# Layer norms with tokens on partitions, and the output product of a second attention taken token by token, in a two-layer transformer block

## The chip, the cores and the metric

The kernel runs on one core of a Trainium2 chip. The metric is the device time of one execution in microseconds (us). An execution with the hardware profiler gives a trace of every instruction on every engine: TensorE (PE, its weight loads PEld), VectorE (DVE), ScalarE (ACT), GpSimd (POOL) and SyncE (SP), which issues transfers.

## The reference, cut to what matters

The input is 4 sequences of 1024 tokens with 128 features. Two layers follow, each `x = x + attention(norm(x)) * silu(feedforward(norm(x)))`, all in fp32:

```
def _layernorm(x, axis=-1, eps=1e-05):
    m = jnp.mean(x, axis=axis, keepdims=True)
    v = jnp.var(x, axis=axis, keepdims=True)
    return (x - m) / jnp.sqrt(v + eps)
...
    xn = _layernorm(x, axis=-1)
    s = _L0_attn_ref(xn, L0_attn_w_kqv)
    g = _silu(_L0_ffn_ref(xn, ...))
    x = x + s * g
    xn = _layernorm(x, axis=-1)
    s = _L1_attn_ref(xn, ...)
    g = _silu(_L1_ffn_ref(xn, ...))
    x = x + s * g
```

The first attention has 16 heads of 8 features and a window of 64 tokens. The first feed-forward mixes the weights of eight experts, per sequence, by a gate that is averaged over the sequence. The second attention runs over the four sequences: each of the 1024 positions has a softmax over 4 tokens t and s per head, and a gated relative bias. The second feed-forward has two input products of 512, two inner products of 512 x 512 and an output product.

## The kernel before

The features lie on the 128 partitions and the tokens along the free axis, so x, its norm xn and all intermediate results are [128, tokens] tiles. A unit u is 512 tokens; there are eight, two for each sequence b.

The program order at the end of `block_kernel` is: the norms of units 0 and 1 and the experts of sequence 0; then for each unit the first attention (four blocks of 128 tokens, each in four groups of four heads), the first feed-forward `ffn0`, the norm for the second layer, and a generator `ffn1` for the second feed-forward, which advances a step at every yield of the next unit's attention. In unit 0 the norms of the other sequences and their experts stand between the blocks. Last comes `attend`, the second attention, in two halves n of 512 positions: its first half advances the last unit's `ffn1`, its second has nothing beside it.

A scheduler, when the program is built, places the instructions of each engine in an order of its own, by estimated costs and data dependencies; the order is fixed from then on, and each engine works through its own in order. Tiles come from pools with a fixed number of buffers: in PSUM four banks "M", two "S", one "T" and one "O"; in SBUF four buffers of every tag of `tmp`, `t2k` among them.

Lines that matter:

- `layernorm`, L153 to L177: centring by a product with I - 1/128 (L156), the square (L158), the copy of the centred values (L160), four products with a column 1/128 that give the variances with tokens on partitions (L163), square root (L165) and reciprocal (L167), a diagonal matrix of the reciprocals made by POOL (L169), its product with ones, which repeats a token's factor on every partition (L176), and the last product (L177).
- `experts`, L179 to L206: the gate (L185, L187, its sum L189) and 16 mixing steps of DVE (L206).
- `attention`: scores (L250), bias (L258), maximum (L262), subtraction on POOL (L263), Exp (L264), totals (L265), transposes (L268), their copy (L270), product with the values (L273).
- `ffn0`: residual on POOL (L303, L304). `ffn1`: L312, L313, the inner products L323, the output product L329, its result into g1 (L330).
- `attend`: projections (L341), gate (L352), scores over 32 partitions per token t (L381), softmax (L392 to L399), the expansion of the probabilities (L409), which reads 32 partitions of t and writes 128, product with the values (L412, L415), sum over s on POOL (L416), output projection (L420), bias and gate (L422), residual (L423), transfer out (L424).
- The transfers at the start (L111 to L124): on SP the constants, the gate, the expert weights tw1, then x1 to x3 and wa; on ACT x0, the attention bias, w1, w2 and tw2.

An fp32 matmul of the program is two MATMUL records of the trace.

Of the kernel before, what the change touches and what calls it, by code (L numbers as in the profile page):

```python
# [27 lines left out]
C_ID, C_CEN, C_ONE, C_AVG, C_MP, C_MF, C_SEL, C_EXP = np.cumsum(  # L28
    [0, 128, 128, 128, 1, 4, 512, 64]
).tolist()  # L30
# [12 lines left out]
def constants():  # L43
# [4 lines left out]
    c[:, C_CEN:C_CEN + P] = np.eye(P) - 1.0 / P  # L48
    c[:, C_ONE:C_ONE + P] = 1.0
    c[:, C_AVG] = 1.0 / P  # L50
# [20 lines left out]
def block_kernel(ctx: ExitStack, tc: tile.TileContext, a: dict, out: bass.AP):  # L71
# [12 lines left out]
    def t2k(tag="t2k"):  # L84
        return tmp.tile([P, 512], F32, tag=tag, name=tag)
# [5 lines left out]
    x = [main.tile([P, S], F32, tag=f"x{b}", name=f"x{b}") for b in range(B)]  # L91
    cst = const.tile([P, C_N], F32, tag="cst", name="cst")
# [19 lines left out]
    nc.scalar.dma_start(out=x[0], in_=a["x"][:, 0:S])  # L112
# [9 lines left out]
    for b in range(1, B):  # L122
        nc.sync.dma_start(out=x[b], in_=a["x"][:, b * S:(b + 1) * S])
# [19 lines left out]
    g1 = main.tile([P, B, S], F32, tag="g1", name="g1")  # L143
# [9 lines left out]
    def layernorm(u):  # L153
        b, cx, cn = tokens(u)
        xc_ps = bank()
        PE.matmul(xc_ps, lhsT=cst[:, C_CEN:C_CEN + P], rhs=x[b][:, cx], start=True, stop=True)  # L156
        sq = t2k()
        ACT.activation(sq, xc_ps, AF.Square)  # L158
        xc = t2k()
        DVE.tensor_copy(xc, xc_ps)  # L160
        var = bank()
        for i in range(4):
            PE.matmul(var[:, i:i + 1], lhsT=sq[:, i * P:(i + 1) * P], rhs=cst[:, C_AVG:C_AVG + 1], start=True, stop=True)  # L163
        std = small([P, 4], "std")
        ACT.activation(std, var[:, 0:4], AF.Sqrt, bias=eps)  # L165
        rstd = small([P, 4], "rstd")
        DVE.reciprocal(rstd, std)  # L167
        diag = t2k()
        POOL.tensor_tensor(  # L169
            diag.rearrange("p (i c) -> p i c", i=4),  # L170
            ident.unsqueeze(1).to_broadcast([P, 4, P]),
            rstd.unsqueeze(2).to_broadcast([P, 4, P]),
            ALU.mult,
        )
        rep = bank()
        PE.matmul(rep, lhsT=ones, rhs=diag, start=True, stop=True)  # L176
        DVE.tensor_tensor(xn[b][:, cn], xc, rep, ALU.mult)  # L177
# [155 lines left out]
    def attend(n, pool):  # L333
# [67 lines left out]


        acc = pool.tile([P, B, U], F32, tag="aq", name="acc")
        for s in range(B):
            eps4 = [bank() for _ in range(B)]
            for half in range(2):
                for t in range(B):
                    rows = slice(32 * t, 32 * t + 32)
                    PE.matmul(eps4[t][:, half * hu:(half + 1) * hu], lhsT=expand[rows, half, :], rhs=pr[rows, s, :], start=True, stop=True)  # L409
            for t in range(B):  # L410
                if s == 0:
                    DVE.tensor_tensor(acc[:, t, :], eps4[t], vv[:, s, :], ALU.mult)  # L412
                else:
                    pv = pool.tile([P, U], F32, tag="pd", name="pd", bufs=8)
                    DVE.tensor_tensor(pv, eps4[t], vv[:, s, :], ALU.mult)  # L415
                    POOL.tensor_tensor(acc[:, t, :], acc[:, t, :], pv, ALU.add)  # L416
            yield
        for t in range(B):
            op = bank("O")
            PE.matmul(op, lhsT=wa[:, 3 * D:4 * D], rhs=acc[:, t, :], start=True, stop=True)  # L420
# [7 lines left out]
    for u in range(2):  # L428
        layernorm(u)
# [14 lines left out]
    for u in range(8):  # L444
        q, k, vv = nxt
        s = at.tile([P, U], F32, tag="s", name="s", bufs=2)
        for t in range(4):
# [3 lines left out]
            if u == 0 and t < 3:  # L451
                for i in range(2):
                    layernorm(2 * (t + 1) + i)
                experts(t + 1)
# [10 lines left out]
        layernorm(u)  # L465
# [72 lines left out]
```

## Time and profile before

| | |
|---|---|
| runs | 2259.92, 1119.83, 1118.67 us; median 1119.83 |
| profiled execution, own time | 2259.92 us (the first of these runs) |
| its span, first to last instruction | 2258.1 us |
| mean granted TensorE clock in it | 1.000 |
| transfers over the span | 14.80 MB |
| ACT table loads | 183 in the program's order, 1.28 us each |

The profiled execution took about twice as long as the two others. Times of rows and stages below are those of the profiled execution; the median is that of the runs.

How to read the profile: its first part gives each engine's busy time, its share of the span and the number of instructions. The chain that ended last follows the work back from the last instruction, at each step to what released it. A row of a group has the line, the engine, the operation, "output<-input" by the program's names, shapes, the number of instructions, then busy time in us and the mean duration in ns, then the idle time of the engine just ahead of them and what ended it. Busy time counts overlapping instructions once, so busy time divided by the number is the time that one occupies. A stage row has its stretch, then busy time and number of instructions of PE, PEld, DVE, ACT and POOL, the granted clock, the transfer engines' share and GB/s. A timeline row has its start, its duration, and in brackets the idle time before it with its releaser.

### The profile page before, as it was taken

To read this page: it belongs to the slowest core of one execution; us is meant where nothing else is said; L and a number is where in the kernel's file an instruction comes from. 1 tells how busy PE (TensorE), PEld (TensorE's weight loads), DVE (VectorE), ACT (ScalarE), POOL (GpSimd) and SP (SyncE) were. 2 spreads that over 40 slices of the span, in tenths; PEclk is the share of its full clock that TensorE was granted. 3 is DMA by queue.
4 is the path that set the end of the run, shared out by engine and by line. 5 is a ranking of instruction groups with operands and counts; after the bars stand their busy time and mean duration, and the time that the engine had idled before them with its cause. 6 is when DMAs were issued, how large, how long until landed. Compare 5 with 4: busy or idle time off the path is not lost.

```text
span 2258.1 us, 11983 instructions
## 1 busy us (share of the span) xinstructions
PE 2173.7 (96%) x4760; PEld 813.0 (36%) x4760; DVE 440.9 (20%) x726; ACT 541.6 (24%) x709; POOL 365.9 (16%) x364
## 2 busy tenths in 40 slices
PE   6998999999999999999999999999999999989995
PEld 3345342343334342334324333434334433332322
DVE  2343411112011201111011201121111201113124
ACT  1221322222122313222122312232222312211010
POOL 2310301022011201121101200120102110011223
DMA  4000100000000000000000000000000000000000
GB/s 161 1 0 0 52 0 0 0 0 0 0 0 0 0 0 0 0 0 1 0 0 0 0 0 1 0 0 0 0 0 1 0 0 0 0 0 0 0 19 19
DMA packets 3959, 14.80 MB, mean 7 GB/s; under 512 B 568, under 2 KB 824, under 8 KB 3264
## 3 DMA queue, kind: packets, MB, share of 16 engines
q1 hardware_dynamic: 3184, 9.85, 1.1%
q10 hardware_dynamic: 720, 4.19, 0.5%
q8 instruction: 37, 0.61, 0.1%
q14 instruction: 18, 0.15, 0.0%
HBM read 11.95 MB, written 2.10 MB: 6 GB/s over the span
## 4 chain that ended last, share of the span: by engine, by line
PE 93%; DVE 2%; POOL 2%; issue 1%; ACT 1%; DMA 0%; POOLq 0%; ACTq 0%; DVEq 0%
PE ps_M L323 27%; PE ps_S L250 15%; PE ps_O L273 12%; PE ps_T L268 6%; PE ps_M L312 3%; PE ps_M L329 3%; PE ps_M L300 3%; PE ps_M L296 3%; PE ps_M L313 3%; PE ps_M L341 3%; PE ps_M L176 2%; PE ps_M L226 2%; PE ps_M L156 1%; PE ps_M L163 1%; PE ps_M L409 1%
## 5 line engine op out<-in xcount | busy, mean ns | idle before, releaser
L323 PE MATMUL ps_M<-hid,l1h 128*128 128x512 f32 x512 | 632.4, 1416 | 0.0
L250 PE MATMUL ps_S<-kb,q 32*64 32x512 f32 x512 | 349.9, 1365 | 21.0 <-DVE pr L258 15.6
L273 PEld LDWEIGHTS ps_O<-pt,vb 128*32 128x32 f32 x2048 | 249.0, 170 | 283.1 <-issue 241.2
L273 PE MATMUL ps_O<-pt,vb 128*32 128x64 f32 x2048 | 307.6, 369 | 12.0 <-ACT pt L270 8.0
L258 DVE TENSOR_TENSOR pr<-ps_S,bias 128x512 f32<-128x512 f32 x128 | 87.4, 686 | 1086.8 <-PE ps_S L250 1071.3
L323 PEld LDWEIGHTS ps_M<-hid,l1h 128*128 128x128 f32 x512 | 159.9, 332 | 316.8 <-issue 311.3
L263 POOL TENSOR_TENSOR pr<-pr,mx 128x512 f32<-128x512 f32 x128 | 132.3, 1040 | 737.3 <-DVE mx L262 727.0
L324 ACT ACTIVATE hid<-ps_M,vec 128x512 f32<-128x512 f32 x64 | 44.0, 687 | 551.5 <-PE ps_M L323 551.5
L268 PE MATMUL ps_T<-cst,pr 128*128 128x128 f32 x512 | 173.5, 503 | 1.8 <-ACT pt L270 1.8
L268 PEld LDWEIGHTS ps_T<-cst,pr 128*128 128x128 f32 x512 | 95.0, 207 | 168.7 <-issue 153.2
L270 ACT COPY pt<-ps_T 128x512 f32<-128x512 f32 x128 | 74.9, 585 | 297.8 <-PE ps_T L268 288.0
L264 ACT ACTIVATE pr<-pr 128x512 f32<-128x512 f32 x128 | 79.3, 627 | 203.0 <-POOL pr L263 202.8
L242 POOL TENSOR_TENSOR vb<-v,cst 128x512 f32<-128x512 f32 x64 | 72.5, 1150 | 237.8 <-PE ps_O L273 171.9
L233 POOL TENSOR_TENSOR kb<-k,cst 128x768 f32<-128x768 f32 x32 | 46.8, 1469 | 374.5 <-PE ps_S L250 308.3
L250 PEld LDWEIGHTS ps_S<-kb,q 32*64 32x64 f32 x512 | 29.5, 134 | 212.8 <-issue 132.4
L264 ACT ACT_TABLE_LOAD x82 | 105.2, 1283 | 1.4
L265 DVE TENSOR_REDUCE total<-pr 128x4 f32<-128x512 f32 x128 | 85.3, 679 | 73.9 <-ACT pr L264 73.9
L262 DVE TENSOR_REDUCE mx<-pr 128x4 f32<-128x512 f32 x128 | 86.1, 682 | 10.7 <-POOL pr L260 4.0
L313 PE MATMUL ps_M<-xn,l1w 128*128 128x512 f32 x64 | 84.7, 1425 | 0.0
L312 PE MATMUL ps_M<-xn,l1w 128*128 128x512 f32 x64 | 82.8, 1396 | 0.0
L329 PE MATMUL ps_M<-hid,l1w 128*128 128x512 f32 x64 | 78.2, 1416 | 0.0
L296 PE MATMUL ps_M<-xn,mw 128*128 128x512 f32 x64 | 78.0, 1440 | 0.0
(112 smaller groups left out, 1321.6 us busy)
## 6 DMA issues: line engine op xcount, KB each, us to landing
tw<-in_tw SPq DMA_DIRECT2D x1, 2048.0 KB, 11.8
tw<-in_tw ACTq DMA_DIRECT2D x1, 2048.0 KB, 14.4
l1h<-in_l1h SPq DMA_DIRECT2D x2, 1024.0 KB, 8.5
out<-t2k SPq DMA_DIRECT2D x8, 256.0 KB, 2.0
x<-in_x SPq DMA_DIRECT2D x3, 512.0 KB, 13.0
bias<-in_bias ACTq DMA_DIRECT2D x1, 1024.0 KB, 8.3
l1w<-in_l1w SPq DMA_DIRECT2D x3, 256.0 KB, 2.9
cst<-in_const SPq DMA_DIRECT2D x1, 610.5 KB, 5.8
```

The lines of the kernel that those rows point to most:

```text
L250: PE.matmul(sp[W * i:W * i + W, :, :], lhsT=q[rows, t * P + W * i:t * P + W * i + W], rhs=kb[rows, :, W * i:W * i + P], start=True, stop=True,
L258: DVE.tensor_tensor(pr, sp, bias[:, 4 * j:4 * j + 4, :], ALU.add)
L262: DVE.tensor_reduce(mx, pr, AX.X, ALU.max)
L263: POOL.tensor_tensor(pr, pr, mx.unsqueeze(2).to_broadcast([P, 4, P]), ALU.subtract)
L264: ACT.activation(pr, pr, AF.Exp)
L268: PE.transpose(tp[:, h, :], pr[:, h, :], ident)
L273: PE.matmul(o[rows, W * i:W * i + W], lhsT=vb[i][:, h, rows], rhs=pt[:, h, W * i:W * i + W], start=(h == 0), stop=(h == 3),)
L296: PE.matmul(hp, lhsT=mw1[b][:, c * P:(c + 1) * P], rhs=xn[b][:, cn], start=True, stop=True)
L312: PE.matmul(p1, lhsT=wt["w1"][:, c * P:(c + 1) * P], rhs=xn[b][:, cn], start=True, stop=True)
L313: PE.matmul(p2, lhsT=wt["w2"][:, c * P:(c + 1) * P], rhs=xn[b][:, cn], start=True, stop=True)
L323: PE.matmul(hp, lhsT=wt[name][:, i, c * P:(c + 1) * P], rhs=hid[:, i, :], start=(i == 0), stop=(i == FC - 1))
L329: PE.matmul(op, lhsT=wt["w3"][:, i, :], rhs=hid[:, i, :], start=(i == 0), stop=(i == FC - 1))
```

## The change

There are two parts. The layer norm first. The input norm (units 0 to 7 of the first layer) reads a second copy of x with tokens on partitions, `xt`, which the host prepares and which is loaded into the tile g1, whose own contents are written only later. The norm between the layers turns x by four TensorE transposes into one M bank. Both then take batch-norm statistics and their aggregation on DVE, square root on ACT, reciprocal and normalisation on DVE, four transposes back into one bank, and a copy to xn on ACT. The centring, variance and diagonal products, the square and POOL's diagonal go.

The second part is in `attend`: the loop over the tokens t is now outside that over s. For each pair, two expansions of the same 32 partitions are followed by the product with the values and an output projection of this product, which accumulates over s in PSUM. The accumulator in SBUF and POOL's additions go, and with them four of the yields.

```
+    g1 = main.tile([P, B, S], F32, tag="g1", name="g1")
+    xt = [g1[:, b, :].rearrange("p (i d) -> p i d", d=P) for b in range(B)]
...
-    nc.scalar.dma_start(out=x[0], in_=a["x"][:, 0:S])
+    nc.scalar.dma_start(out=g1[:, 0, :], in_=a["xt"][:, 0:S])
...
     for b in range(1, B):
+        nc.sync.dma_start(out=g1[:, b, :], in_=a["xt"][:, b * S:(b + 1) * S])
+    for b in range(B):
         nc.sync.dma_start(out=x[b], in_=a["x"][:, b * S:(b + 1) * S])
...
-    def layernorm(u):
+    def layernorm(u, src):
+        b, _, cn = tokens(u)
+        stats = small([P, 4, 6], "stats")
+        mv = small([P, 4, 2], "mv")
+        for i in range(4):
+            DVE.bn_stats(stats[:, i, :], src[:, i, :])
+        for i in range(4):
+            DVE.bn_aggr(mv[:, i, :], stats[:, i, :])
         std = small([P, 4], "std")
+        ACT.activation(std, mv[:, :, 1], AF.Sqrt, bias=eps)
         rstd = small([P, 4], "rstd")
         DVE.reciprocal(rstd, std)
+        nt = t2k()
+        nt = nt.rearrange("p (i d) -> p i d", i=4)
+        for i in range(4):
+            DVE.tensor_scalar(nt[:, i, :], src[:, i, :], mv[:, i, 0:1], rstd[:, i:i + 1], ALU.subtract, ALU.mult)
+        back = bank()
+        for i in range(4):
+            PE.transpose(back[:, i * P:(i + 1) * P], nt[:, i, :], ident)
+        ACT.copy(xn[b][:, cn], back)
+
+    def layernorm_in(u):
+        layernorm(u, xt[u // 2][:, 4 * (u % 2):4 * (u % 2) + 4, :])
+
+    def layernorm_mid(u):
+        b, cx, _ = tokens(u)
+        turned = bank(shape=(P, 4, P))
+        for i in range(4):
+            at = cx.start + i * P
+            PE.transpose(turned[:, i, :], x[b][:, at:at + P], ident)
+        layernorm(u, turned)
...
-        acc = pool.tile([P, B, U], F32, tag="aq", name="acc")
-        for s in range(B):
-            eps4 = [bank() for _ in range(B)]
-            for half in range(2):
-                for t in range(B):
-                    rows = slice(32 * t, 32 * t + 32)
-                    PE.matmul(eps4[t][:, half * hu:(half + 1) * hu], lhsT=expand[rows, half, :], rhs=pr[rows, s, :], start=True, stop=True)
-            for t in range(B):
-                if s == 0:
-                    DVE.tensor_tensor(acc[:, t, :], eps4[t], vv[:, s, :], ALU.mult)
-                else:
-                    pv = pool.tile([P, U], F32, tag="pd", name="pd", bufs=8)
-                    DVE.tensor_tensor(pv, eps4[t], vv[:, s, :], ALU.mult)
-                    POOL.tensor_tensor(acc[:, t, :], acc[:, t, :], pv, ALU.add)
-            yield
         for t in range(B):
+            rows = slice(32 * t, 32 * t + 32)
             op = bank("O")
-            PE.matmul(op, lhsT=wa[:, 3 * D:4 * D], rhs=acc[:, t, :], start=True, stop=True)
+            for s in range(B):
+                ep = bank()
+                for half in range(2):
+                    PE.matmul(ep[:, half * hu:(half + 1) * hu], lhsT=expand[rows, half, :], rhs=pr[rows, s, :], start=True, stop=True)
+                pv = pool.tile([P, U], F32, tag="pd", name="pd", bufs=8)
+                DVE.tensor_tensor(pv, ep, vv[:, s, :], ALU.mult)
+                PE.matmul(op, lhsT=wa[:, 3 * D:4 * D], rhs=pv, start=(s == 0), stop=(s == B - 1))
```

The built order after the change has, in the first half of `attend`, four expansions of one token, two projections, and again four and two, with four matmuls of L323 between tokens; in the second half expansions and projections alone. It has 175 ACT table loads. On DVE the statistics of units 2 to 4, which read xt1 and xt2, stand ahead of the gate's sum of sequence 0.

## The prediction

> **What bounds the kernel now.** I read the times, the busy shares, a table of five stages, the chain that ended last, the groups by shape, then the timeline of the last 40 us. First lines of the page:
>
> ```profile
> span 2258.1 us, 11983 instructions
> PE 2173.7 (96%) x4760; PEld 813.0 (36%) x4760; DVE 440.9 (20%) x726; ACT 541.6 (24%) x709; POOL 365.9 (16%) x364
> PE 93%; DVE 2%; POOL 2%; issue 1%; ACT 1%; DMA 0%; POOLq 0%; ACTq 0%; DVEq 0%
> ```
>
> In this execution TensorE is the bound almost everywhere. But it took 2259.92 us, and two other runs of the program took 1119.83 and 1118.67. DVE, ACT and POOL sum to 1348 us, overlapped, so half the time can only come from the matmuls: with r the share of their profiled durations that the shorter runs need, 2173.7 r must fit into 1118.67, so r is at most 0.515. Every sum is made twice, in the profile's time and in the median's.
>
> Stages, from the stage table (stretch, PE busy, PE weight loads, DVE, ACT, POOL):
>
> ```profile
> 38.00:238.00 200.00, 183.92 (x566) 95.80 (x567) 87.84 (x156) 45.85 (x77) 43.97 (x44) 1.00 0.00 1
> 238.00:2040.00 1802.00, 1774.73 (x3748) 646.93 (x3750) 280.49 (x470) 468.15 (x595) 260.08 (x263) 1.00 0.01 2
> 2040.00:2190.00 150.00, 149.98 (x248) 45.39 (x240) 36.95 (x48) 17.92 (x23) 31.33 (x24) 1.00 0.02 7
> 2190.00:2258.00 68.00, 43.31 (x169) 14.79 (x168) 30.78 (x40) 3.87 (x5) 26.54 (x21) 1.00 0.04 16
> ```
>
> They are: the first unit with six layer norms and three experts; seven units of attention and feed-forward; second attention's first half, mixed with feed-forward; its second half, alone. With PE times r the first is close to DVE's 88 us, the second and third stay TensorE's with idle gaps, and the last is a chain.
>
> [...] The trace has two records per fp32 matmul (512 at L323 for 256 in the program)[...]. I take r = 0.40, with 0.35 and 0.515 as ends. [...] an L409 record, four row groups in turn, occupies 28.5/128 = 0.22 us, and L219, full height, 23.1/32 = 0.72 us for 288 columns. [...]
>
> **The change part by part.** Price rows:
>
> ```profile
> L156 PE MATMUL ps_M<-x,cst 128*128 128x512 f32 x32 | 42.1, 1407 | 10.4 <-DMA x<-in_x 6.8 <-POOL x L304 3.5
> L176 PE MATMUL ps_M<-t2k,cst 128*128 128x512 f32 x32 | 41.9, 1411 | 6.5 <-POOL t2k L169 6.5
> L163 PE MATMUL ps_M<-cst,t2k 128*128 128x1 f32 x128 | 38.0, 418 | 4.4 <-ACT t2k L158 4.4
> L268 PE MATMUL ps_T<-cst,pr 128*128 128x128 f32 x512 | 173.5, 503 | 1.8 <-ACT pt L270 1.8
> L219 PE MATMUL ps_M<-xn,wqkv 128*128 128x288 f32 x32 | 23.1, 905 | 0.0
> L409 PE MATMUL ps_M<-apr,cst 32*128 32x256 f32 x128 | 28.5, 805 | 9.2 <-DVE apr L399 8.4 <-DVE acc L412 0.9
> L420 PE MATMUL ps_O<-acc,wa 128*128 128x512 f32 x16 | 21.2, 1425 | 5.5 <-DVE t2k L422 2.8 <-POOL acc L416 2.7
> ```
>
> *Layer norm.* Out: (42.1 + 41.9 + 38.0)/16 = 7.6 us of PE each. In: four transposes at 173.5/512 = 0.34, so 1.4 us, for each of eight input norms; eight, 2.7 us, for each of eight middle norms. PE saves 6.2 and 4.9 us. DVE loses a copy, a reciprocal and a product (0.685 + 0.171 + 0.688 = 1.54) and gains four statistics, four aggregations, a reciprocal and four normalisations. The trace shows no batch-norm instruction: a statistic lies between L435's 0.15 (eight elements) and L289's 0.29 (128), I take 0.28 because it reads 128; an aggregation 0.16; a normalisation 0.28 (L191 0.274). Sum 3.05, so DVE +1.5 us, ends +1 and +1.6. ACT swaps a square (0.60) for a copy (0.59) and has eight table loads fewer (183 to 175, 1.28 each); POOL loses 1.04. The chain from x to xn has two hops fewer and about equal work; I give it nothing. A middle norm keeps one M bank until its last normalisation; other users of M in that stretch wait for xn anyway.
>
> *Waits added.* In each middle norm the statistics wait on DVE for PE's transposes, which wait for POOL's residual add; behind them stand a maximum and two totals of attention, for which POOL's subtraction and PE's transposes wait. Before, the copy L160 stood in that queue with the same wait, so the wait is moved and not new; only its length (eight short instructions against one) is, and it is in the 1.5 us. The result's copy now waits on ACT for four transposes; behind it stands a copy of attention's transposed weights, for which PE's L273 waits. Before, L158's square stood there with a wait of its own. In second attention a projection waits on PE for DVE's product (0.69) right behind the expansions: one or two more expansions stand between, 0.5 us or more at r = 0.40, so a few tenths per pair are open, inside the 1 us of the tail and the range.
>
> *Head.* SP issues three xt loads where x1 to x3 stood, then four x loads, 2 MB more, needed first at the residual add (261 us in the profile); only wa is behind them, needed after 2000 us. The DVE order puts statistics of xt1 ahead of the first normalisation, and x1 landed at 17.3 us: first xn near 20 us, gate sum near 27 against 35.5 us. Profile -7.6; at r = 0.40 the old chain ends near 24, the new near 23: -1.
>
> *First unit.* Six norms: PE -37 in the profile. At r = 0.40 PE saves 15 but DVE, as busy there, gains 9, partly under waits that go: -3, ends -12 and +9.
>
> *Middle norms.* Eight times -4.9 = -39; at r = 0.40 -15.7, of which I count -12 since PE idles there part of the time; ends -24 and -4.
>
> *Second attention, per half.* The expansion's 64 records lose their neighbours in other row groups, the token's loop now being outermost: 64 x 0.642 (L219 scaled to 256 columns) = 41.1 against 14.2, +26.9. The output projection goes from 4 to 16 matmuls: 24 records more at 1.325, +31.8. POOL loses 12 adds of 1.27 us, DVE nothing. First half: +58.7; at r = 0.40 +23.5, less about 2 that L420 waits for the adds: +21. The order keeps feed-forward matmuls between tokens; gaps could take more.
>
> *Second half.* Old, from the timeline:
>
> ```profile
> 2221.28 2.60 PE L409 MATMUL ps_M<-apr,cst 32*128 32x256 f32 x16 [8.38 <-DVE apr L399]
> 2228.35 14.71 POOL L416 TENSOR_TENSOR acc<-acc,pd 128x512 f32<-128x512 f32 x12 [22.92 <-DVE pd L415]
> 2239.46 2.63 PE L420 MATMUL ps_O<-acc,wa 128*128 128x512 f32 x2 [2.67 <-POOL acc L416]
> 2253.75 1.26 POOL L423 TENSOR_TENSOR t2k<-t2k,x 128x512 f32<-128x512 f32 x1 [2.34 <-DVE t2k L422]
> ```
>
> From probabilities to the end: 36.8 us. The reader sees POOL's adds carry it, which do not shrink with r: 4.3 + 14.7 + a projection 1.06 + 0.75 + 1.26 + 3.1 to the end = 25-26. New: PE carries it: 64 x 0.642 + 32 x 1.325 = 83.5, and about 5 after the last matmul: 88.5, +51.7 in the profile; at r = 0.40 33.4 + 1 + 5.1 = 39.5, +13. VectorE's 16 products (11 us) hide under it.
>
> Sum in the profile: -7.6 - 37 - 39 + 58.7 + 51.7 = +27, 2260 to 2287. At r = 0.40: -1 - 3 - 12 + 21 + 13 = +18, 1119.8 to **1138**. Own range 1124 to 1152.
>
> **The rivals.** *Gaps take it.* TensorE is the bound of the profiled execution only; at 0.35 it is busy 761 us of 1119, so the first half's extra fits gaps (+8), the tail costs +10, middle norms give all of -24 with the shorter chain, the first unit -12, the head -2: 1100. Against: the third stage has 150 us of PE beside at most 37 of any other engine. *The serial product is fully exposed.* One mechanism, in second attention: r near 0.5, no gap free: +29 and, with the old tail at 28.5 and the new at 48, +19; the norms return only -5 and -1: 1162. It decides once PE in the shorter runs exceeds about 0.45 of the profile's; for it, the chain's 93%. *VectorE becomes the bound.* Thirteen short instructions in order ahead of attention's products: first unit +9, middle norms -4, head -1, attention +34: 1158. Against: DVE is busy 280 of 1802 us in the middle. That the change does not do what it says is excluded for the order of instructions, which is fixed at build: four matmuls of one token stand together, then two projections.
>
> **How the numbers follow.** Forecast 0.48, gaps 0.15, serial 0.22, VectorE 0.15. Two per cent, about what a measurement of this kernel can tell from no change, is 1097 to 1142. Faster: half of gaps, 0.07. Slower: 0.15 of the forecast's 0.48, 0.20 of serial, 0.09 of VectorE, 0.44. Same: 0.49. The range takes in gaps and serial with their bounds: 1104 to 1172.
>
> **What would show it.** Right: expansion records about 0.64 us apart if matmuls take as long as in this profile, about 0.26 at r = 0.40, against 0.22 now; no POOL add in the tail; the tail from probabilities near 40 us; statistics near 0.28. Wrong: expansions of different tokens overlapping, the statistics holding DVE's queue before attention's products, the xt wait starting the gate later than before, or r outside 0.35 to 0.515.

## The result, and the profile after

The changed kernel takes 1132.48 us (median of 4 runs, 1127.72 to 1134.09) against 1119.25 beside it (median of four, the run of 2259.92 us among them): a ratio of 1.0114, 95% interval 1.0075 to 1.0152. It is slower, by less than the two per cent that count as a difference. The forecast was 1138. The ratios are estimated from the single runs and are not quotients of the medians.

Two things have to be known before the numbers are read. The profile of before was taken in an execution of twice the usual time; the kernel before was therefore run again (first experiment below), and stages are compared with that profile, whose span is 1118.3 us. And the mean clock granted to TensorE differs between executions of one kernel, from 0.865 to 0.883 of full speed in that repeat, and the time goes with it, 1126 down to 1109 us; so a difference of a few us in a long stage that TensorE fills is not read as an effect of the edit.

The page of the changed kernel, the same three lines as in the prediction (span, busy time, chain that ended last):

```profile
span 1130.4 us, 11985 instructions
PE 1001.9 (89%) x4712; PEld 492.7 (44%) x4712; DVE 459.1 (41%) x886; ACT 523.5 (46%) x701; POOL 331.3 (29%) x324
issue 5%; POOL 1%; POOLq 0%
```

TensorE is busy 89% of the span. The chain says nothing this time: it breaks off after the last 6%. So the stages have to carry the comparison. Stage table of the changed kernel (columns as in the prediction: stretch, PE, PE weight loads, DVE, ACT, POOL, granted clock):

```profile
20.30:149.00 128.70, 98.59 (x529) 59.49 (x529) 95.60 (x215) 37.63 (x73) 41.85 (x38) 0.70 0.12 50
149.00:937.60 788.60, 738.88 (x3598) 356.50 (x3598) 275.83 (x522) 441.54 (x569) 251.53 (x249) 0.90 0.00 1
1001.70:1048.10 46.40, 46.31 (x129) 23.04 (x130) 14.11 (x21) 3.35 (x4) 5.06 (x4) 0.96 0.06 21
1083.30:1130.40 47.10, 41.11 (x96) 19.82 (x96) 14.03 (x21) 0.00 (x0) 5.06 (x4) 0.75 0.06 23
```

The same four stretches of the kernel before, run again:

```profile
26.60:163.80 137.20, 105.67 (x578) 61.19 (x576) 84.71 (x155) 46.53 (x79) 43.09 (x43) 0.75 0.00 1
163.80:951.20 787.40, 747.20 (x3627) 359.34 (x3626) 274.84 (x462) 440.81 (x569) 254.56 (x257) 0.90 0.01 4
1020.20:1045.60 25.40, 22.91 (x97) 10.35 (x98) 9.95 (x17) 3.34 (x4) 13.48 (x11) 0.93 0.00 1
1084.70:1118.30 33.60, 21.19 (x72) 11.46 (x72) 12.94 (x20) 0.00 (x0) 19.73 (x16) 0.50 0.08 31
```

They are the first unit, seven units, the first half of second attention from its probabilities, and the second half from its probabilities. The first is 8.5 us shorter, the second the same although TensorE is busy 8 us less, the third 21.0 longer and now full of TensorE, the fourth 13.5 longer. Where each us went, with three of the experiments beside it (us from one event to the next, worked out from the traces):

| stage | before again | after | norms alone | attention alone | input norms alone |
|---|---|---|---|---|---|
| start to the first gate product | 26.6 | 20.3 | 20.5 | 26.9 | 20.6 |
| to the first `ffn0` | 137.2 | 128.7 | 127.4 | 137.0 | 124.7 |
| seven units, to the last `ffn0` | 787.4 | 788.6 | 781.1 | 784.0 | 783.7 |
| to the gate of second attention | 42.3 | 37.5 | 37.5 | 42.3 | 39.8 |
| to the probabilities, first half | 26.7 | 26.6 | 26.7 | 26.6 | 26.7 |
| to the end of the last `ffn1` | 25.4 | 46.4 | 25.4 | 46.4 | 23.7 |
| to the gate of the second half | 13.7 | 10.2 | 13.6 | 10.2 | 13.7 |
| to its probabilities | 25.4 | 25.0 | 25.4 | 25.0 | 25.4 |
| to the end | 33.6 | 47.1 | 33.4 | 47.3 | 33.4 |

The gains lie at the start (-6.3 and -8.5) and before second attention (-4.8); the losses in second attention (+21.0 - 3.5 - 0.4 + 13.5). With +1.2 in the units that is +12, the difference of the two spans. The row of the seven units shows how far a long stage can be trusted: "after" and "norms alone" do the same work there and take 788.6 and 781.1 us, at mean clocks of 0.90 and 0.91.

Four of the price rows in the kernel before, run again (busy time, mean ns of one):

```profile
L323 PE MATMUL ps_M<-hid,l1h 128*128 128x512 f32 x512 | 248.5, 613 | 1.6 <-DVE acc L412 0.8
L156 PE MATMUL ps_M<-x,cst 128*128 128x512 f32 x32 | 30.0, 1037 | 16.2 <-POOL x L304 9.5
L409 PE MATMUL ps_M<-apr,cst 32*128 32x256 f32 x128 | 19.6, 550 | 10.7 <-DVE apr L399 9.5 <-DVE acc L412 0.8
L420 PE MATMUL ps_O<-acc,wa 128*128 128x512 f32 x16 | 12.3, 861 | 6.3 <-POOL acc L416 3.5 <-DVE t2k L422 2.8
```

Rows of the changed kernel that answer the price rows:

```profile
L172 PE MATMUL ps_M<-cst,t2k 128*128 128x128 f32 x64 | 21.1, 418 | 20.5 <-DVE t2k L169 20.5
L185 PE MATMUL ps_M<-cst,x 128*128 128x128 f32 x32 | 7.9, 394 | 10.0 <-POOL x L313 10.0
L159 DVE BATCH_NORM_STATS2 stats<-g 128x6 f32<-128x128 f32 x32 | 7.3, 272 | 15.9 <-DMA g<-in_xt 15.9
L416 PE MATMUL ps_M<-apr,cst 32*128 32x256 f32 x128 | 36.8, 447 | 9.5 <-DVE apr L408 9.5
L419 PE MATMUL ps_O<-pd,wa 128*128 128x512 f32 x64 | 39.0, 737 | 0.8 <-DVE pd L418 0.8
```

The statistic takes 272 ns; it overlaps its neighbours and occupies 7.3/32 = 0.23 us, where 0.28 was forecast. With all that VectorE does in a norm, it is busy 2.77 us per norm instead of 1.53, so +1.2 where +1.5 was forecast. An expansion record occupies 36.8/128 = 0.29 us; in the kernel before, run again, it was 19.6/128 = 0.15. These averages mix two halves with different clocks. In the first half, at stage clocks of 0.93 and 0.96, it went from 0.10 to 0.25 us, close to the forecast's scaled 0.09 and 0.26; in the second, at 0.50 and 0.75, from 0.20 to 0.32. Its neighbours no longer work in other row groups (in the first profile 59 of the 128 records of L409 start within 0.015 us of the one before; those of L416 in the first half mostly start 0.22 us apart). Of the 64 records of the projection 48 are new work; they occupy 0.61 us each on average, and follow each other by 0.43 where the clock is full.

The last 47 us of the changed kernel in the timeline, first token (start, duration):

```profile
1083.40 2.92 PE L416 MATMUL ps_M<-apr,cst 32*128 32x256 f32 x6 [8.37 <-DVE apr L408]
1086.25 2.08 PE L419 MATMUL ps_O<-pd,wa 128*128 128x512 f32 x2
```

There is no POOL sum any more (the stage row shows POOL with the 4 residuals alone, 5.06 us); TensorE goes from expansion to projection. But the two records of a projection take 2.08 us here, and in the first half about 1.0. The clock of 0.75 is a mean: it is 0.50 in this trace until 1106.7 us, for almost half of the stage, and 1.00 from there to the end. The records tell the same: projection records that follow each other directly start 0.85 us apart up to then, and 0.43 afterwards.

### The profile page after: what moved, and what is told of

Same layout as the page of the kernel before. It is cut to its first block, busy times and chain, and to the rows that moved or that the text cites. A ratio compares the mean times of both kernels' runs of the same rounds, so it can differ in the third digit from the quotient of the medians.

```text
span 1130.4 us, 11985 instructions
## 1 busy us (share of the span) xinstructions
PE 1001.9 (89%) x4712; PEld 492.7 (44%) x4712; DVE 459.1 (41%) x886; ACT 523.5 (46%) x701; POOL 331.3 (29%) x324
## 5 line engine op out<-in xcount | busy, mean ns | idle before, releaser
L332 PE MATMUL ps_M<-hid,l1h 128*128 128x512 f32 x512 | 246.4, 609 | 0.0
L259 PE MATMUL ps_S<-kb,q 32*64 32x512 f32 x512 | 184.2, 726 | 35.1 <-DVE pr L267 24.4
L282 PEld LDWEIGHTS ps_O<-pt,vb 128*32 128x32 f32 x2048 | 137.4, 122 | 125.6 <-issue 51.1
L282 PE MATMUL ps_O<-pt,vb 128*32 128x64 f32 x2048 | 163.8, 240 | 21.5 <-ACT pt L279 21.4
L332 PEld LDWEIGHTS ps_M<-hid,l1h 128*128 128x128 f32 x512 | 88.8, 190 | 99.5 <-issue 94.0
L251 POOL TENSOR_TENSOR vb<-v,cst 128x512 f32<-128x512 f32 x64 | 84.9, 1352 | 98.5 <-PE ps_O L282 74.9
L277 PE MATMUL ps_T<-cst,pr 128*128 128x128 f32 x512 | 99.4, 323 | 3.6 <-ACT pr L273 3.6
L277 PEld LDWEIGHTS ps_T<-cst,pr 128*128 128x128 f32 x512 | 68.8, 162 | 67.9 <-issue 41.2
L242 POOL TENSOR_TENSOR kb<-k,cst 128x768 f32<-128x768 f32 x32 | 46.6, 1467 | 152.1 <-PE ps_S L259 111.3
L416 PE MATMUL ps_M<-apr,cst 32*128 32x256 f32 x128 | 36.8, 447 | 9.5 <-DVE apr L408 9.5
L418 DVE TENSOR_TENSOR pd<-ps_M,av 128x512 f32<-128x512 f32 x32 | 22.1, 692 | 48.3 <-PE ps_M L416 48.3
## 6 DMA issues: line engine op xcount, KB each, us to landing
x<-in_x SPq DMA_DIRECT2D x4, 512.0 KB, 12.6
```

The lines of the kernel that those rows point to most:

```text
L251: POOL.tensor_tensor(m, vv[:, 2 * t + i, :].unsqueeze(1).to_broadcast([P, 4, D]), mfree, ALU.mult)
L259: PE.matmul(sp[W * i:W * i + W, :, :], lhsT=q[rows, t * P + W * i:t * P + W * i + W], rhs=kb[rows, :, W * i:W * i + P], start=True, stop=True,
L277: PE.transpose(tp[:, h, :], pr[:, h, :], ident)
L282: PE.matmul(o[rows, W * i:W * i + W], lhsT=vb[i][:, h, rows], rhs=pt[:, h, W * i:W * i + W], start=(h == 0), stop=(h == 3),)
L332: PE.matmul(hp, lhsT=wt[name][:, i, c * P:(c + 1) * P], rhs=hid[:, i, :], start=(i == 0), stop=(i == FC - 1))
```

## The experiments

Ratios are to the kernel before, run in the same job, with the 95% interval. Of each edit a few lines are shown, with "..." for others; "-" and "+" are against the kernel before or the changed kernel, as each case says.

**The kernel before again** (no edit). 

> The kernel before, unchanged, for a profile of an execution that takes about as long as the median. Forecast's theory: about 1119 us, fp32 matmul records of 512 columns 429 ns apart where the first profile had 1106 (as in the kernel after), the tail from the probabilities to the end 25 to 26 us and carried by the additions on GpSimd, a gap at TensorE ahead of each middle norm. Rival that gaps take it: TensorE idle well over 20 us in second attention's first half. Rival that the serial product is fully exposed: almost no idle time there.

1124.65 us (18 runs), ratio 1.0025 [0.9984, 1.0065]. Nothing of the double time of the first execution came back; a record of the inner products of `ffn1` (L323) occupies 248.5/512 = 0.485 us in it instead of 632.4/512 = 1.235. For this line the share r that the forecast worked with is therefore 0.39, where 0.40 was taken; over all of TensorE it is 991.5/2173.7 = 0.456. TensorE is idle 2.5 of the 25.4 us of second attention's first half, so there are no gaps for the rival *Gaps take it* to fill. The tail was expected to take 25 to 26 us and takes 33.6.

**The norms alone.** The new norms, second attention as before (against the changed kernel):

```
-            for s in range(B):
-                ep = bank()
...
+        acc = pool.tile([P, B, U], F32, tag="aq", name="acc")
+        for s in range(B):
+            eps4 = [bank() for _ in range(B)]
```

> Only the layer norms changed, second attention as before. Forecast's theory (TensorE saves 16 us of the path): 1103 us, that is 0.986 of before. Rival that VectorE becomes the bound: +4 us, 1123. Rival that gaps take it: norms give 38 us, 1081. Serial rival: norms return only 6, 1113.

1092.47 us, ratio 0.9771 [0.9716, 0.9826]: faster than before by 1.7 to 2.8%. This lies between the forecast's theory (1103) and the rival of the gaps (1081), and rules out the other two (1113 and 1123). The norms gain more than the forecast's 16 us. By the stage table 15.9 us are gained up to the first `ffn0`, 4.8 after the last, and 6.3 in the seven units; of those 6.3 the clock can make as much as the whole, since the changed kernel, with the same norms, gains nothing there.

**Second attention alone.** The old norms, the new `attend` (against the kernel before):

```
-        acc = pool.tile([P, B, U], F32, tag="aq", name="acc")
-        for s in range(B):
...
+                PE.matmul(op, lhsT=wa[:, 3 * D:4 * D], rhs=pv, start=(s == 0), stop=(s == B - 1))
```

> Only second attention's output changed, the layer norms as before. Forecast's theory: +34 us, 1153. Rival that gaps take it: +18, 1137. Rival that the serial product is fully exposed: +48, 1167. VectorE rival: +34. If the two parts are independent, this difference and that of the norms alone add up to the +13 of the whole change.

1149.84 us, ratio 1.0314 [1.0221, 1.0407]: +25 to +46 us, so the forecast's +34 holds and the +18 and +48 of two rivals do not. The two parts of the change add up within these intervals: -2.3% and +3.1% against +1.1% together. Stage by stage the changed kernel is the norms-alone column up to second attention, apart from the seven units, and the attention-alone column from there.

**The order alone.** Second attention token by token, but with POOL's sum and one projection per token (against the kernel before):

```
+        for t in range(B):
+            rows = slice(32 * t, 32 * t + 32)
+            op = bank("O")
...
+                    POOL.tensor_tensor(acc, acc, pv, ALU.add)
+            PE.matmul(op, lhsT=wa[:, 3 * D:4 * D], rhs=acc, start=True, stop=True)
```

> The kernel before with one thing changed in second attention: the token's loop is outermost, so that expansions of the same 32 partitions follow each other, but the sum over s stays on GpSimd and there is one output projection for each token. First half (from the probabilities to the end of feed-forward's output product): old 25.4 us; 64 expansion records one after another at 216 ns, as in the kernel after, in place of groups of four: about +7, so 32. Tail: old 33.6; 64 records in a row beside the additions, about 34 if TensorE's clock stays low there, 28 if the projections now overlap the additions. Whole: +7 (1127), or +1 with the shorter tail. Rival that the order alone carries the loss: +20 or more. Rival that gaps take it: 0.

**The projections alone.** The loop over s outside and the row groups side by side as before, but each product goes straight into the projections, which add up in four PSUM banks (against the kernel before):

```
+        ops = [bank("O"), bank("T"), bank("S"), bank("S")]
...
-                    POOL.tensor_tensor(acc[:, t, :], acc[:, t, :], pv, ALU.add)
+                PE.matmul(ops[t], lhsT=wa[:, 3 * D:4 * D], rhs=pv, start=(s == 0), stop=(s == B - 1))
```

> The kernel before with the other thing changed: s stays outermost, expansions of four row groups together, but each product goes straight into an output projection that accumulates in one of four PSUM banks (O, T and both S), with no sum on GpSimd. First half: 12 more projections at 0.86 us: +10, less 3.5 for the projections that no longer stand among the next half's input projections: +7 in all. Tail: old 33.6; if TensorE's clock stays as low as in the old tail (0.5), 16 projections of 2.05 us give about 40; if it recovers, 16 at 0.86 and the expansions give about 25. Whole: from -2 to +13, 1118 to 1133. Rival that the projections carry the whole loss of the change in second attention: +30.

The order alone: 1138.36 us, ratio 1.0161 [1.0083, 1.0240]. The projections alone: 1132.40 us, ratio 1.0106 [1.0050, 1.0161]. The last stage of the order alone:

```profile
1096.40:1137.20 40.80, 32.23 (x72) 19.69 (x72) 13.83 (x21) 0.00 (x0) 20.19 (x16) 0.50 0.07 26
```

and of the projections alone:

```profile
1094.30:1126.40 32.10, 22.18 (x96) 9.93 (x96) 12.66 (x20) 0.00 (x0) 4.93 (x4) 0.82 0.09 33
```

So in the last stage the loss needs the order: 33.6 to 40.8 us with 72 records as before, and 47.1 with projections and order together; the projections by themselves cost nothing there (32.1 us), although they are 24 records more. They take the place of POOL's sum, and the stage was granted 0.82 of the clock instead of 0.50; how much each of the two does is not separated. In the first half, where other matmuls are waiting, both cost: 25.4 to 44.0 us with the order, to 37.3 with the projections, to 46.4 with both; 3.4 to 3.5 us of this come back in the next stage each time. An expansion record occupies 0.28 us there with the order alone and 0.10 with the projections alone, so its price is the order's. The two losses do not add. With the order alone the projections also wait for POOL's sums, which accumulation in PSUM takes away, but only for 2.4 us in this half; its clock there was 0.81 instead of 0.96, and what makes the rest is not settled. The order was expected to cost 7 us and cost 18 by the ratio; the projections were expected between -2 and +13, and cost 12.

**The input norms alone.** The norm between the layers as before, the input norms new (the tile of the statistics with two buffers; against the kernel before):

```
     for u in range(2):
-        layernorm(u)
+        layernorm_in(u)
...
         ffn0(u, s)
-        layernorm(u)
+        layernorm_old(u)
```

> Only the input norm is changed; the norm between the layers and second attention are as before. (The statistics tile has two buffers in place of four, for room.) By the stages of the profiles: the input norm's part is what comes ahead of the first feed-forward, -15 us, so 1105; the middle norms' part, -5 to -11, is missing. Forecast's theory as written: -4 from head and first unit, so 1116. VectorE rival: the first unit longer by 9, 1128.

1093.12 us, ratio 0.9758 [0.9704, 0.9811]: the time of the norms alone to 0.7 us, and less than the 1105 and 1116 expected here. At a clock of 0.875 two runs took 1093.9 and 1092.8 us, and one of the norms alone 1092.1. The eight middle norms, half of the change in the norms, are worth nothing that can be measured, where each of the two times is known to about 6 us.

That is not because they save nothing. In the seven units TensorE is busy 745.8 us with the input norms alone and 729.4 with all: -16.4, or -2.3 for each of the seven middle norms there, where -2.0 was forecast. (The norms' own matmuls go from 40.2 to 19.5 us; the others take 5.9 longer.) What it waits for, though, in the stretch from 165 to 925 us (columns: us in total, times, longest), with the input norms alone:

```profile
PE ps_S L289 <- DVE pr L297: 13.3, 19, 0.8
PE ps_O L312 <- ACT pt L309: 13.2, 6, 2.6
PE ps_T L307 <- ACT pr L303: 1.4, 3, 0.6
```

and with all norms new (scores, product with the values, transposes of the probabilities):

```profile
PE ps_S L259 <- DVE pr L267: 20.9, 19, 3.3
PE ps_O L282 <- ACT pt L279: 15.2, 6, 2.6
PE ps_T L277 <- ACT pr L273: 4.0, 7, 0.6
```

Attention's matmuls wait 7.6 + 2.0 + 2.6 = 12.2 us longer. Three quarters of what the middle norms save is returned as waits. The largest, 3.3 us, occurs three times, behind the norms of units 1, 3 and 5. One of them in the timeline of the norms alone:

```profile
270.88 0.89 DVE L159 BATCH_NORM_STATS2 stats<-ps_M 128x6 f32<-128x128 f32 x4 [1.11 <-PE ps_M L185]
272.82 1.47 POOL L242 TENSOR_TENSOR kb<-k,cst 128x768 f32<-128x768 f32 x1 [1.15 <-PE ps_S L259]
274.57 0.69 DVE L271 TENSOR_REDUCE mx<-pr 128x4 f32<-128x512 f32 x1 [2.51 <-POOL pr L269]
277.09 1.96 PE L259 MATMUL ps_S<-kb,q 32*64 32x512 f32 x2 [3.29 <-DVE pr L267]
```

TensorE's gap runs from 273.80 to 277.09 us. VectorE stands idle for 2.51 us up to 274.57, at a maximum that waits for POOL's fill of the masked corner (L269), which stands on POOL behind the masked keys (L242), which wait for TensorE. Only then does it work off that maximum, two totals and the bias addition that frees the bank of the next scores. With the old middle norm, in the trace of the input norms alone, the fill (268.94 us) stood ahead of the keys (271.11) and the bias addition (271.06) ahead of the maximum (271.67). So the new norm came with another built order; that its durations led the scheduler to it is likely and not shown.

**Statistics twice.** The norms alone, with each of the 64 statistics done twice (against the changed kernel):

```
         for i in range(4):
             DVE.bn_stats(stats[:, i, :], src[:, i, :])
+        for i in range(4):
+            DVE.bn_stats(stats[:, i, :], src[:, i, :])
```

> Both norms changed, second attention as before, and every batch-norm statistic is computed twice: 4 x 0.21 us (start to start) more on VectorE in each norm, 13 us in all. If VectorE is the bound in the first unit (VectorE rival), head and first unit grow by 6 to 7 us there and middle norms by most of 7: 1106. If VectorE's extra work hides, within 3 us of the norms alone: 1092 to 1096.

1101.31 us, ratio 0.9823 [0.9754, 0.9892], 8.8 us above the norms alone by the medians and 5.8 by the ratios, with the intervals overlapping; two runs at a clock of 0.875 took 1096.6 and 1098.3 us, and the norms alone at 0.875 took 1092.1. The extra statistics are 14.4 us of busy time, if they cost what the first ones do (7.3 + 7.1). In size this is inconclusive. But the built order changed again, and that bears on the waits of 3.3 us. In this trace, with more work on VectorE in every norm, TensorE's scores wait 11.3 us for the bias additions in the same stretch instead of 20.9, and never longer than 0.8: behind the norm of unit 1 a product with the values now stands ahead of those scores. The clock was halved at this place in both traces (six records of scores take 1.98 us), so it is not the clock that makes the difference. VectorE's own work in the norm is therefore not enough to make the waits of 3.3 us; it takes the order as well. Part of the wait moved elsewhere (the product with the values waits 21.2 us instead of 15.2), and this kernel was not faster than the norms alone.

**TensorE kept busy before and in the last stage.** The kernel before, with 24 extra matmuls in the second half (against the kernel before):

```
+        if n == 1:
+            busy(m1, 2)
...
+                    if n == 1:
+                        busy(pv, 1)
```

Here `busy(src, k)` multiplies a matrix of ones with `src` k times, into a bank that nothing reads.

> The kernel before, with 24 extra matmuls in the second half of second attention, from the maxima of the scores to the last product, where TensorE otherwise waits for VectorE and GpSimd; nothing reads their results. Theory: the last stage (probabilities to end, 33.6 us in the kernel before) is 8 us longer than forecast because TensorE is granted only 0.50 of its clock there, so that a projection takes 2.05 us. Kept busy it gets 0.75 or more, a projection takes 1.0 to 1.4 us, four of them stand for -3 to -4 us, the expansions for -1 more: last stage 28 to 30 us, time -4 to -6. Rival: the 2.05 us come from something else (weights, bank, semaphores): projections stay at 2.0 us, and the stage is the same or 1 to 3 us longer because of the extra matmuls.

1124.04 us, ratio 1.0051 [1.0009, 1.0093]. The granted clock in the last stage (from 1086.4 us) rises from 0.50 to 0.90, and the price in dispute falls. A projection of the kernel before, run again:

```profile
1105.07 2.05 PE L420 MATMUL ps_O<-acc,wa 128*128 128x512 f32 x2 [0.93 <-DVE t2k L422]
```

and the same projection beside the extra matmuls:

```profile
1108.62 1.10 PE L436 MATMUL ps_O<-acc,wa 128*128 128x512 f32 x2 [0.94 <-DVE t2k L438]
```

2.05 us become 1.02 to 1.10 (1.68 for the last of the four): the clock makes this price, as the theory had it. That it makes the 8 us by which the stage exceeds the forecast is not borne out: the expected 28 to 30 us did not come. The stage takes 33.2 us instead of 33.6, and its probabilities come 3.5 us later. The extra matmuls stand in order before the next expansions, so that POOL's sums come in groups 5.6 us apart with 0.7 us of idle time between, where they followed each other without a gap (12 in 14.72 us). And from the end of the last sum to the end of the kernel it takes 11.4 us instead of 12.6, only 1.2 less with projections at half the price, because the four projections still take turns in the one bank O.

**The second sequence's load early.** The norms alone, with `xt1` (the second sequence's tokens, which the expectation calls the second token's) loaded ahead of the gate weights (against the changed kernel):

```
+    nc.sync.dma_start(out=g1[:, 1, :], in_=a["xt"][:, S:2 * S])
...
-    for b in range(1, B):
+    for b in range(2, B):
```

> The norms alone (second attention as before), with the second token's transposed input loaded ahead of the gate weights instead of behind everything the first unit needs. Theory: after the new norms what stands last in the head is the wait of VectorE for this load, 8.4 us idle up to 17.0 us; with the load early the first gate matmul comes at 12 to 15 us instead of 20.3 and the time falls by 5 to 8 us against the norms alone (1092.5), to about 1085. Rival: the loads share the DMA engines, so that the load of the gate weights or of the expert weights is late by as much and the time is within 2 us of 1092.5.

1102.65 us, ratio 0.9846 [0.9765, 0.9927], 10 us above the norms alone. The first gate product came at 15.0 us instead of 20.5, as expected, and the second unit's at 26.6 instead of about 22. Up to 15.0 us the transfer engines were busy 0.90 of the time and moved 342 GB/s. The load that VectorE waits for is now the next one:

```profile
23.89 0.87 DVE L160 BATCH_NORM_STATS2 stats<-g 128x6 f32<-128x128 f32 x4 [8.93 <-DMA g<-in_xt]
```

8.9 us for `xt2` in place of 8.5 for `xt1`; and on ScalarE a square root that waits for these statistics stands ahead of the second copy to xn, so that the gate's sum (29.6 us instead of 25.2) and the first mixing step (31.4 instead of 26.8) are later than without the edit. Neither theory had this: the built order asks for the next load before it has landed. The first `ffn0` starts 2.8 us later, at 150.7 us. The code from there on is the same. At like clocks (0.876 and 0.877 against 0.878) this kernel took 1099.8 and 1096.7 us and the norms alone 1092.1 and 1092.8, so 4 to 8 us of the 10 are not the clock's, and what makes them beside the 2.8 is open.

**Products into the projection in the second half only**, with the early load (against the changed kernel):

```
+        else:
+            ops = [bank("O"), bank("T"), bank("S"), bank("S")]
...
+                    PE.matmul(ops[t], lhsT=wa[:, 3 * D:4 * D], rhs=pv, start=(s == 0), stop=(s == B - 1))
```

> The norms alone with the early load, and in the second half only the products go straight into the output projection, which adds them up in four PSUM banks (the first half as before). Theory: where nothing else runs, the projections on TensorE and the sum on GpSimd are about equal (32.1 against 33.6 us measured apart), so -1 to -2 us against the early load alone. Rival: the clock in the last stage follows how busy TensorE is; with 16 projections in place of 4 it could rise to 0.75 or 1.0, and the stage shorten by 5.

**The same with 12 extra matmuls ahead of the probabilities**, whose results nothing reads (against the changed kernel):

```
+        if n == 1:
+            busy(m1, 2)
```

> The same, with 12 extra matmuls ahead of the probabilities of the second half, whose results nothing reads. Theory (clock): the last stage starts at a higher clock, 26 to 28 us against 32, time -4 to -6 against the version without them. Rival: 16 projections keep the clock up by themselves and the extra matmuls change nothing or cost 1 us.

1097.81 us, ratio 0.9811 [0.9748, 0.9874], and 1099.20 us, ratio 0.9804 [0.9740, 0.9868]. The last stage is 31.2 us in the first (33.4 with the early load alone) at a clock of 0.88: the clock rose as the rival had it, the stage shortened by about as little as the theory had. In the second it is 28.8 at 0.93, of which 1.3 are lost again ahead of the probabilities; 26 to 28 was expected. Neither gain shows in the medians. None of these was measured faster than the norms alone, whose median is the lowest of all versions.

**The mask's fill on VectorE.** The norms alone, with this (against the changed kernel):

```
-                POOL.memset(pr[0:W, :, 0:W], NEG)
+                DVE.memset(pr[0:W, :, 0:W], NEG)
```

> The norms alone, with the masking fill of attention's first block in the even units done by VectorE instead of GpSimd, right behind the bias addition. In the norms-alone kernel the seven middle norms save 16 us of TensorE and the seven units are 2.6 us shorter at most; after the odd units' norms TensorE stands 3.3 us for the bias addition, 0.8 with the old middle norms. Theory: not the norm's own arithmetic but an order that it brings about costs this: on VectorE a maximum stands ahead of the next bias addition and waits for GpSimd's fill, which stands behind the masked keys, which wait for TensorE. With the fill on VectorE the three waits of 3.3 us fall to about 1, the seven units from 781 to 772-776 and the time by 5 to 8 us, to about 1085 to 1087. Rival: the wait is VectorE's own work of the norm (2.5 us per norm): then the waits stay near 3 us, and the fills (16 of some 0.2 us) add 0 to 3 us, 1092 to 1095.

1099.59 us (1088.56 to 1113.55), ratio 0.9769 [0.9714, 0.9824]. The waits behind the odd units' norms:

```profile
PE ps_S L259 <- DVE pr L267: 16.3, 20, 1.6
```

The longest is 1.6 us instead of 3.3, three times, and the sum 16.3 instead of 20.9, with VectorE doing more and not less; about 1 was expected. VectorE no longer stands at the maximum: maximum, total, fill and bias addition follow each other. So the stall at POOL's fill is gone. How much of the halving is owed to this is not separated, since TensorE's clock just ahead of these three places was 1.00 in this trace and 0.50 to 0.53 in that of the norms alone. The expected 1085 to 1087 us did not come, and that the shorter waits give time back is not shown: the ratio is that of the norms alone, and the runs had clocks from 0.851 (the trace) to 0.876, which moves the time by more than the 5 us at stake.

## Why the prediction was right, and where its steps were not

The time, 1132.48, lies 5.5 us below 1138 and inside the forecast's own range. The signs of both parts were right. The sum is close because misses cancel: head and first unit gained 14.8 us where 4 were forecast, the middle norms nothing that was measured where 12 were, and second attention lost 30.6 us where 34 were. That these cancel is luck.

*Scale.* One share r for all matmuls was the weakest step: 0.40 and the lower end 0.35 were the author's estimates, which nothing in the first profile shows; 0.515 follows from its busy time. L323 shows 0.485/1.235 = 0.39, but all of TensorE's busy time 991.5/2173.7 = 0.456, and the rows that this change is about shrank least: L156 to 0.71 of its first profile, L409 to 0.69, L420 to 0.58. The old norm's three products cost (30.0 + 28.8 + 25.0)/16 = 5.2 us a norm, not 7.6 x 0.40 = 3.0; the transposes that replace them take 1.3 us in an input norm and 2.3 in a middle norm. So TensorE saves 3.9 and 2.9 us a norm, where 2.5 and 2.0 were counted. The rival that needed 0.35 falls with this. The serial rival asked for more than about 0.45, which was just met; it fails on its sums.

*Head*, -1 forecast, -6.3 measured: right mechanism, mis-sized term. The chain to the gate's sum was taken to end near 24 us before and near 23 after; it ended at 30.7 and at 25.0. (In the profile's time the step's own figures, 27 against 35.5, give -8.5 and not the -7.6 that its sum uses.) The new chain:

```profile
16.98 0.68 DVE L159 BATCH_NORM_STATS2 stats<-g 128x6 f32<-128x128 f32 x3 [8.38 <-DMA g<-in_xt]
17.89 2.13 DVE L169 TENSOR_SCALAR t2k<-g,mv,rstd 128x128 f32<-128x128 f32 x8
```

The wait for x1's load is there as forecast (17 us); but eight normalisations behind it take 2.13 us, 0.27 each, and the transposes of two units 2.27, so that the chain behind it is short. The old chain had the centring product, the diagonal's and the second unit's centring on TensorE, of 2.07, 2.08 and 1.91 us, which the forecast had scaled by 0.40 to 1.1 each. They are as long as the projections that took 2.05 us at a clock of 0.50.

*First unit*, -3 forecast, -8.5 measured. The step counted busy time, PE -15 against DVE +9, and took most of both as hidden. VectorE did gain 10.9 us of work (95.6 instead of 84.7), but waits that went with the old norms were larger: in the repeated kernel it waited 14.5 us for the repeated factors (L177 for L176) in this stretch and 5.3 for the gate's sum; after the change the first is gone and the second 0.2, while its longest wait, for attention's scores, grew from 16.3 to 22.5. The rival in which VectorE's extra work costs 9 us here is wrong in sign.

*Middle norms*, -12 forecast, nothing measured: the runs with all norms and with the input norms alone differ by 0.7 us. The step failed where it said that a wait "is moved and not new". TensorE saved its 16 us, and 12 came back as attention's waits, with the order in which VectorE and POOL take attention's instructions as the one cause that was traced. The rival *VectorE becomes the bound* had named that queue and left the middle norms 4 of their 12 us, which is nearer. But in the gap that was traced VectorE had been idle for 2.51 us and was late by its order, and in a kernel with still more work in every norm and another order these gaps were gone.

*Second attention, first half*, +21 forecast: +21.0 to the end of the last `ffn1`, -3.5 after it, since the output projections are done by then: +17.5. The terms were right as well as the sum: the expansions take 9.6 us more (10.8 forecast) and the projections 13.3 more (12.7).

*Second half*, +13 forecast (25.5 to 39.5), +13.5 measured (33.6 to 47.1): the difference is right and both ends are 8 us too low. In the old stage POOL's sums end at 21.0 us where 19.0 was forecast; the step put the last projection right behind them, but it starts 5.3 us later, at 1111.03: the four share the single bank O and stand 2.98 us apart. This queue is the larger part of the old stage's 8 us. The clock is the smaller: with the extra matmuls the sums began 1.5 us sooner after the first expansion, and what follows the last sum was 1.2 us shorter. In the new stage 33.4 us of TensorE were forecast, and 41.1 are busy, while the same instructions take 32.8 us in the first half: there the excess is the clock, 0.50 for half of the stage. The trace of the changed kernel has the two prices: a record of a projection is 0.85 us from the next in the first part of the last stage, where the clock is 0.50, and 0.43 in the rest of it, where the clock is 1.00. When it rises is not settled: with the extra matmuls it was 0.90 in the old stage, but here TensorE was busy 22.1 of the 23.0 us from 1083.3 to 1106.3 us, and the clock stayed at 0.50. Since both ends were missed by the same amount for different reasons, the right difference is luck too.

*Serial product fully exposed*, +29 and +19: the first half is exposed indeed (46.31 of 46.40 us busy), but at a clock of 0.96 and so at +21, the second half lost 13.5, and the norms returned more than 6.

*The range.* It was said to take in the rival of the gaps, but begins at 1104, above that rival's 1100.

*Shown and not shown.* Shown by experiment: that the two parts of the change add up within their intervals; that the input norms carry the gain of the norms, with times known to about 6 us; that the expansions' price comes from the order of the loops; that the clock makes the price of a projection in the last stage; that the waits of 3.3 us need the built order and are not VectorE's work alone. Not settled: what makes the rest of the 12 us of longer waits, what the waits are worth in time (two kernels with shorter waits for the bias addition were not faster), and when the clock rises.

## What to carry to other kernels

Time that one engine saves in a stretch with three others in a chain may stay a gap, as 12 of 16 us did here; find out which wait on that engine grew before counting it. A short instruction may owe its price to its neighbours: taking the loop over row groups out of the innermost place raised an expansion from 0.10 to 0.25 us. A stage at the end of a kernel is priced with the records of that stage, with its queues for a single buffer included: a projection took 2.05 us there and about 1.0 in the busy middle. And a profile of unusual length can't be scaled by one factor: here the factor went from 0.39 to 0.71 by line.

## What the runs showed of the hardware

- The time of one kernel goes with its mean granted clock: 1107.75 us at 0.881 and 1126.30 at 0.865 for the kernel before. Time times clock lies between 971 and 980 in its 41 runs of that job.
- In the trace of the changed kernel every clock record is 0.5 or 1.0, and the 49 stretches ahead of the last are multiples of 3.413 us, from 3.4 to 78.5; a stage clock such as its 0.75 is a mixture of the two.
- A batch-norm statistic over 128 elements takes 272 ns from SBUF and 286 from PSUM, four in 0.84 to 0.89 us; an aggregation 153 ns, four in 0.36.
- A normalisation of 128 elements takes about 0.34 us from SBUF and 0.40 from PSUM. In the changed kernel five of the eight from SBUF that ran beside POOL took 0.92 to 1.30 us, and each ended 0.08 us after a product or subtraction of POOL that ran beside it. From PSUM none did, though 16 of 32 ran beside POOL.
- Expansions one after another in one row group took 1.99 us for 8 in the first half, 0.25 each, with their weight loads (1.59 us for the 8) beside them.
- In the first execution TensorE was busy 2.2 times as long as in the repeat, and the inner products L323 2.5 times. Its trace has no clock records at all, so the 1.000 printed for it is not a measured clock. Why it was slow is open.
